# Sixteen-head attention in a decoder: VectorE's instructions pinned to the order of the text, with four of them moved

## The chip, the cores and the metric

The kernel runs on one core of a Trainium2 chip. The metric is the device time of one execution in microseconds (us), the median of three runs. The engines of the core are named as the profile names them: PE is the matrix engine (PEld its weight loads), DVE the vector engine, ACT the scalar (activation) engine, POOL the general one, SP the engine that issues most of the transfers. Each engine works through its own list of instructions in order, and engines wait for each other through semaphores. Matrix products land in PSUM[...].

## The reference

Twelve layers follow each other on x, which is 8 x 256 x 256 (batch, position, width) in float32: four times a self-attention, a cross-attention to a context, and a feed-forward part. After each, x becomes layernorm(x + part). The self-attentions of layers 0, 3 and 6 have 16 heads of width 16, and they are what the change is in; that of layer 9, with heads of width 64, is another function:

```python
# layer 0, 3 and 6, per batch entry and head (d = 16)
s = (q @ k.T) * 0.25          # 0: plain; 3: plus a bias linear in the distance; 6: causal mask
a = softmax(s)                # exp(s - max) / sum
y = concat_heads(a @ v) @ wo  # layers 0 and 3 have biases, layer 0 and 3 also bo
x = layernorm(x + y)
```

## The kernel before

`attention16` computes one such layer; it is called for layers 0 (`kind="bias"`), 3 (`"alibi"`) and 6 (`"causal"`). The work is cut in 16 blocks, `(b, c)`: eight batch entries, and for each the two halves c of eight heads. A block has four steps, s = 0 to 3. `step(i, s)` does two things at once: for the next block i + 1 the scores of four head pairs with queries as rows (tile `s`), from which DVE takes the maximum of each row (line 409; in the causal layer a mask addition, line 401, and two maxima, lines 404 and 406), and for the block i itself the scores with keys as rows (tile `t`), from which the maximum has been taken off already inside the product, and of which ACT makes exponentials (`eT`, line 415). The maxima of a block are collected in `nm`, turned by PE (`ntr`) and put into the queries by `less_max` (`qm`, line 434, two instructions). `attend` multiplies the exponentials with the values and with columns of ones (`av`): the first half of `av` holds the result, the second the sums. `normalise` (lines 462 and 463) takes the reciprocal of the sums and multiplies.

`s` and `t` come from one pool of two buffers of two PSUM banks each, and alternate. So the product `s` of a step can't start before DVE has taken the maximum of the step before it, and `t` not before ACT has made that step's exponentials. The other four banks are two called `av` and two called `mm`; the projections (`pk`, `pq`, `pv`), the output projection `po`, and both kinds of transposes (`ntr`, `xtr`) take turns in the two `mm` banks.

Between the steps stands work of other batch entries: in a block with c = 0 the projections `pk` and `pq` of the next entry and, after step 3, `leave` of the previous entry, which is the output projection (`project_out`, y at line 294) and the norm; in a block with c = 1 the rest of the previous block's attention, `normalise`, the projection `pv`, and `finish` of the previous entry, which transposes the new x for the next layer (`transpose_x`, copied out of PSUM by `evac`).

The norm of one entry is a chain over two engines: DVE makes statistics (lines 158 and 159, two halves of the entry), POOL makes the reciprocal of the deviation (lines 161 and 163), and DVE scales (line 181, two instructions).

The order of PE's instructions in this stage is that of the text: `in_order` ties each matmul and transpose to the one before it, from `chain[:] = [True, None]` to `chain[:] = [False, None]`. All other engines' instructions are put in order by the scheduler of the framework, from its own estimates. `evac` sends every third copy of the whole kernel to ACT and the others to DVE, by a count that runs on through all layers (`turn`).

## Time and profile before

| | |
|---|---|
| median of 3 runs | 4036.28 us (4034.14 to 4036.88) |
| the profiled execution | 4028.63 us, of which the span from first to last instruction is 4026.7 us |
| mean granted PE clock over the span | 0.952 |
| PE busy in 0 to 240 us (layer 0) | 203.16 us; DVE 138.62, ACT 90.07, POOL 23.51; clock 0.95 |
| PE busy in 1055 to 1310 us (layer 3) | 219.11 us; DVE 171.63, ACT 67.70, POOL 15.80; clock 0.91 |
| PE busy in 1955 to 2230 us (layer 6) | 229.04 us; DVE 183.57, ACT 82.85, POOL 62.72; clock 0.90 |

The page gives shares of the whole span; the change concerns these three stretches, so the stretches are what to look at. In them PE is busy most of the time but not all of it, and the clock is below 1. Where a row has "[idle before <-releaser]", the engine stood still for that long before the row, until the named engine had done the named thing.

### The profile page before, as it was taken

Reading aid. Unit: us, or ns where it says so; the run is one execution under the profiler, and the core shown is the slowest. Engines: PE = TensorE matmul, PEld = TensorE weight load, DVE = VectorE, ACT = ScalarE, POOL = GpSimd, SP = SyncE. Lnnn points to the kernel's source line nnn. Section 1 sums busy time; section 2 is a strip of 40 time slices with the busy share of each in tenths; the row PEclk is TensorE's granted clock in tenths of the full one; section 3 lists DMA queues with packets and bytes.
Section 4 is the critical chain, followed back from the end, with each engine's and each line's share of the span. In section 5 each row is a group of like instructions: output and inputs, shape, how many; then the busy total and the mean of one; then the engine's idle time right before and its main releaser. Section 6 shows DMA issues by size and latency. Waiting matters only on the chain.

```text
span 4026.7 us, 51285 instructions
## 1 busy us (share of the span) xinstructions
PE 3652.1 (91%) x21150; PEld 2595.8 (64%) x21150; DVE 1794.2 (45%) x3431; ACT 1057.0 (26%) x2524; POOL 838.3 (21%) x877
## 2 busy tenths in 40 slices
PE   7889999999988787777788999999999999999997
PEld 5557555555555554666655666677776776778886
DVE  4654222222576675111476446766665444420002
ACT  3321111111122232222232332143333333321111
POOL 1000000000000554100122331032223333332213
PEclk9998999999998898788898999999999999999998
DMA  7000000000000000322100400000001000035542
GB/s 258 1 14 7 16 16 16 32 21 15 20 1 12 17 3 21 132 91 89 45 1 1 87 1 22 29 1 1 1 1 40 11 1 11 11 123 183 183 143 64
DMA packets 64714, 175.70 MB, mean 44 GB/s; under 512 B 7808, under 2 KB 39297, under 8 KB 52129
## 3 DMA queue, kind: packets, MB, share of 16 engines
q0 software_dynamic: 16512, 98.38, 6.7%
q1 hardware_dynamic: 47968, 74.05, 6.2%
q8 instruction: 166, 2.72, 0.3%
q14 instruction: 68, 0.55, 0.0%
HBM read 139.12 MB, written 33.29 MB: 43 GB/s over the span
## 4 chain that ended last, share of the span: by engine, by line
PE 43%; DVE 5%; issue 1%; POOL 1%; ACT 1%; another core or an unknown queue 0%; DMA 0%; POOLq 0%; DVEq 0%; ACTq 0%
PE pq L140 4%; PE po L140 4%; PE pv L140 4%; PE ph L1362 4%; PE py L1369 4%; PE s L577 4%; PE av L603 4%; PE pk L140 3%; PE etr L537 3%; PE py_s L1369 1%; PE py L710 1%; PE ph_s L1362 1%; PE ph L725 1%; PE t L140 1%; DVE s L401 1%
## 5 line engine op out<-in xcount | busy, mean ns | idle before, releaser
L529 POOL TENSOR_TENSOR ex<-ex,urc 128x1024 f32<-128x1024 f32 x192 | 363.8, 1895 | 790.5 <-DVE urc L528 709.5
L525 ACT ACTIVATE ex<-s,nm 128x256 f32<-128x256 f32 (+1 forms) x704 | 338.6, 495 | 408.9 <-DVE nm L520 367.5
L415 ACT ACTIVATE eT<-t 128x1024 f32<-128x1024 f32 (+1 forms) x192 | 182.9, 954 | 423.4 <-PE t L140 423.3
L140 PE MATMUL s<-qk,qk 32*128 32x256 f32 (+1 forms) x1536 | 225.5, 414 | 50.4 <-DVE nm L409 42.5
L520 DVE TENSOR_REDUCE nm<-s 128x4 f32<-128x1024 f32 (+1 forms) x192 | 234.1, 1220 | 71.6 <-PE s L577 67.6
L725 PE MATMUL pu<-xT_l,w2a 128*128 128x512 f32 x512 | 244.4, 600 | 0.0
L725 PE MATMUL pg<-xT_l,w2a 128*128 128x512 f32 x512 | 240.8, 592 | 0.0
L851 DVE TENSOR_TENSOR h<-pu,sg 128x512 f32<-128x512 f32 x128 | 88.5, 692 | 337.8 <-PE pu L725 337.7
L140 PE MATMUL t<-qm,qk 32*128 32x256 f32 (+1 forms) x1536 | 213.8, 401 | 23.9 <-DVE nm L406 22.3
L710 PE MATMUL py<-w2b,h 128*128 128x256 f32 x1024 | 226.2, 379 | 0.0
L850 ACT ACTIVATE sg<-pg 128x512 f32<-128x512 f32 x128 | 76.4, 598 | 566.3 <-PE pg L725 566.3
L710 PEld LDWEIGHTS py<-w2b,h 128*128 128x128 f32 x1024 | 194.6, 190 | 40.1 <-issue 15.3
L537 PE MATMUL etr<-ident,ex 128*128 128x128 f32 x1536 | 210.1, 279 | 10.4 <-issue 4.1
L537 PEld LDWEIGHTS etr<-ident,ex 128*128 128x128 f32 x1536 | 169.2, 141 | 71.1 <-issue 57.3
L140 PEld LDWEIGHTS s<-qk,qk 32*128 32x128 f32 x1536 | 130.6, 199 | 125.6 <-DVE nm L409 60.8
L409 DVE TENSOR_REDUCE nm<-s 128x4 f32<-128x1024 f32 x128 | 156.2, 1223 | 107.5 <-PE t L140 78.7
L603 PE MATMUL av<-eT,vg 128*64 128x256 f32 x1280 | 193.1, 394 | 11.4 <-DVE eT L150 10.0
L161 POOL TENSOR_SCALAR ve_l<-mv_l 128x2 f32<-128x2 f32 x104 | 23.3, 224 | 848.8 <-DVE mv_l L159 848.3
L1082 PE MATMUL ph<-xT_l,w 128*128 128x256 f32 x512 | 135.3, 431 | 65.2 <-DMA w<-in_L_ffn_w,row 65.2
L577 PE MATMUL s<-kg,qg 64*128 64x256 f32 x1280 | 190.6, 404 | 2.1 <-DVE eT L150 1.3
L717 DVE SCALAR_TENSOR_TENSOR x<-py,g,x 128x256 f32<-128x256 f32 x256 | 110.2, 479 | 166.1 <-PE py L710 165.9
L725 PEld LDWEIGHTS pu<-xT_l,w2a 128*128 128x128 f32 x512 | 98.1, 192 | 122.1 <-issue 121.9
(337 smaller groups left out, 6690.6 us busy)
## 6 DMA issues: line engine op xcount, KB each, us to landing
slots<-zero SPq DMA_DIRECT2D x16, 1024.0 KB
given<-yo SPq DMA_DIRECT2D x23, 256.0 KB
w2a<-in_L_ffn_Wg SPq DMA_DIRECT2D x8, 512.0 KB
w2a<-in_L_ffn_Wu SPq DMA_DIRECT2D x8, 512.0 KB
w2b<-in_L_ffn_Wd SPq DMA_DIRECT2D x8, 512.0 KB
lines<-w9r SPq DMA_DIRECT2D x1, 4096.0 KB
bias<-lines SPq DMA_DIRECT2D x4, 768.0 KB
x<-in_x SPq DMA_DIRECT2D x8, 256.0 KB
```

Source lines behind the costliest of these rows:

```text
L140: in_order(nc.tensor.matmul(*args, **kw))
L415: nc.scalar.activation(eT[:, :, :n], tt[:, :, :n], AF.Exp)
L520: nc.vector.tensor_reduce(nm[:, :nseg], flat, AX.X, ALU.max, negate=True)
L525: nc.scalar.activation(ex[:, g, :], flat[:, g, :], AF.Exp, bias=nm[:, g:g + 1], accum_out=sums[:, g:g + 1])
L529: nc.gpsimd.tensor_tensor(ex, ex, rc[:, :nseg].unsqueeze(2).to_broadcast([P, nseg, n]), ALU.mult)
L537: nc.tensor.transpose(tr[:, i // 4, (i % 4) * P:(i % 4 + 1) * P], blk, ident)
L577: nc.tensor.matmul(st[:, i, q * S:(q + 1) * S], qg[r:r + d, c, q * P:(q + 1) * P], kg[r:r + d, c, :], start=True, stop=True)
L603: nc.tensor.matmul(av[64 * i:64 * i + d, c * S:(c + 1) * S], vg[:, k, (2 * c + i) * d:(2 * c + i + 1) * d], eT[:, (2 * i + k) * S:(2 * i + ...
L710: nc.tensor.matmul(py[:, q * D:(q + 1) * D], h[:, f, i * P:(i + 1) * P], w2[:, f, :], start=(f == 0), stop=(f == nf - 1))
L725: nc.tensor.matmul(ph, w1[:, c, f * P:(f + 1) * P], xT[p][:, c, :], start=(c == 0), stop=(c == 1))
L1362: nc.tensor.matmul(ph[:, i * S:(i + 1) * S], w1[:, c, f * P:(f + 1) * P], srcs[c], start=(c == 0), stop=(c == 1))
L1369: nc.tensor.matmul(py[:, q * D:(q + 1) * D], h[:, f, q * P:(q + 1) * P], w2[:, f, :], start=(f == 0), stop=(f == NF - 1))
```

## The change

Five edits, all in effect only inside `attention16`:

1. Inside the stage each DVE instruction is tied to the one before it in the text, as PE's are (`order_of_text` names both engines, and `dve` is a wrapper that records each call). The text is rearranged to the order that is wanted.
2. The norm is cut in `norm_stats` and `norm_scaled`. The scaling of an entry is issued after the maximum of step 0 of the next block, no longer before it. The addition of x (`add_x`) stands between the two instructions of `less_max`, the statistics behind the second.
3. `normalise` works on halves of 128 columns: the first half stands in front of a step's maximum (`first` in `step`), the second behind it. For blocks with c = 0 this is step 1 of the block that follows, for blocks with c = 1 step 0 of the block that follows.
4. The copies out of PSUM of `pk`, `pq` and `pv` are issued one step later than their products (`leave_qk`, `leave_v`).
5. The copy of the transposed x goes to ACT always, and takes no turn in the count of `evac`.

PE's instructions in the three layers, and their order, are the same as before.

```diff
+    @contextmanager
+    def order_of_text(*engines):
+        chains.update({e: None for e in engines})
+        yield
+        chains.clear()
...
+        if chains:
+            nc.scalar.copy(dst, src)
+        else:
+            evac(dst, src)
...
+    def norm_stats(b, y, name):
+        return (b, y) + rstd_of([y[:, q, :] for q in range(NT)], f"{name}_{b}")
+
+    def norm_scaled(of):
+        b, y, mv, rs = of
+        for q in range(NT):
+            dve.tensor_scalar(xs[b][:, q, :], y[:, q, :], mv[:, q, 0:1], rs[:, q:q + 1],
+                                    ALU.subtract, ALU.mult)
...
                 for group in products:
                     for o, l, r in group:
                         matmul(o, l, r, start=True, stop=True)
+                first()
...
-                av = avs.pop(i)
-                rc = wk.tile([P, S], F32, tag="rc", name=f"rc_{li}_{b}_{c}")
-                nc.vector.reciprocal(rc, av[:, S:])
-                nc.vector.tensor_tensor(aTs[b][:, c, :], av[:, :S], rc, ALU.mult)
...
+                av = avs[i]
+                lo, hi = half * P, (half + 1) * P
+                rc = wk.tile([P, P], F32, tag="rc", name=f"rc_{li}_{b}_{c}{half}", bufs=4)
+                dve.reciprocal(rc, av[:, S + lo:S + hi])
+                dve.tensor_tensor(aTs[b][:, c, lo:hi], av[:, lo:hi], rc, ALU.mult)
...
+                for i, (b, c) in enumerate(blocks):
+                    more = b + 1 < B
+                    if c == 0:
+                        step(i, 0, lambda: normalise(i - 1, 0))
+                        normalise(i - 1, 1)
+                        if more:
+                            pk = project_qk(b + 1, 1)
+                        step(i, 1)
+                        if more:
+                            leave_qk(b + 1, 1, pk)
+                            pq = project_qk(b + 1, 0)
+                    else:
+                        step(i, 0)
+                        if b > 0:
+                            norm_scaled(ys.pop(b - 1))
+                        attend(i - 1, 1, (1,))
+                        step(i, 1, lambda: normalise(i - 1, 0))
+                        normalise(i - 1, 1)
+                        if more:
+                            pv = proj_tok(wv, xTb(b + 1), 0, f"pv_{li}_{b + 1}")
+                    step(i, 2)
                     if more:
+                        if c == 0:
+                            leave_qk(b + 1, 0, pq)
+                        else:
+                            leave_v(b + 1, pv)
+                    attend(i, 0, (0, 1))
+                    step(i, 3)
+                    if b > 0:
+                        if c == 0:
+                            po = project_out_mm([aTs.pop(b - 1)], wo, f"{li}_{b - 1}")
+                        else:
+                            finish(b - 1, f"l{li}", last)
+                    if i + 1 < len(blocks):
+                        tr = turn_maxima(i + 1)
+                        less_max(i + 1, 0, tr)
+                    if b > 0 and c == 0:
+                        y = add_x(wk, b - 1, po, bo, f"{li}_{b - 1}")
+                    if i + 1 < len(blocks):
+                        less_max(i + 1, 1, tr)
+                    if b > 0 and c == 0:
+                        ys[b - 1] = norm_stats(b - 1, y, f"l{li}")
+                    attend(i, 1, (0,) if c == 0 else (0, 1))
```

## The prediction

> **What bounds the kernel now.** The page first: its shares and its clock row.

> ```profile
> span 4026.7 us, 51285 instructions
> ...
> PE 3652.1 (91%) x21150; PEld 2595.8 (64%) x21150; DVE 1794.2 (45%) x3431; ACT 1057.0 (26%) x2524; POOL 838.3 (21%) x877
> ...
> PEclk9998999999998898788898999999999999999998
> ```

> PE sets the end nearly everywhere, so time can be won in two ways only: PE stands still less, or it is granted its clock more. The change acts in three stretches (layer 0, about 20 to 277 us; layer 3, 1054 to 1310; layer 6, 1960 to 2218), and there the clock row is lowest. So next, who PE waits for, in the even part of each stretch (90 to 235, 1100 to 1273, 2005 to 2180 us):

> ```profile
> PE s L140 <- DVE nm L409: 12.9, 11, 2.1
> ...
> PE s L140 <- DVE nm L409: 15.2, 13, 2.1
> ...
> PE t L140 <- DVE nm L406: 19.3, 12, 2.5
> ```

> Columns: us in total, times, longest. PE waits for DVE's maximum, because it frees the buffer of the next product. Third, the timeline of layer 0 around the longest of these waits, DVE and PE:

> ```profile
> 103.69 0.48 DVE L434 SCALAR_TENSOR_TENSOR qm<-ntr,hc,qk 128x256 f32<-128x256 f32 x1
> 104.08 0.74 DVE L158 BATCH_NORM_STATS2 st_l<-y 128x6 f32<-128x256 f32 x2
> ...
> 105.19 0.17 DVE L159 BATCH_NORM_AGGREGATE mv_l<-st_l 128x2 f32<-128x6 f32 x1
> 106.51 0.73 DVE L181 TENSOR_SCALAR x<-y,mv_l,rs_l 128x256 f32<-128x256 f32 x2 [1.15 <-POOL rs_l L163]
> 107.16 1.22 DVE L409 TENSOR_REDUCE nm<-s 128x4 f32<-128x1024 f32 x1
> ...
> 108.44 0.64 PE L140 MATMUL s<-qk,qk 32*128 32x256 f32 x2 [2.08 <-DVE nm L409]
> ```

> The scores were ready at 105.33, but DVE, in order, waits 1.15 us for POOL's part of the norm, scales for 0.73, and only then takes the maximum; PE has nothing from 106.36 on. Last, the clock around it, by windows of 3.4 us (us; busy us of PE, PEld, DVE, ACT, POOL; PE clock; DMA share; GB/s):

> ```profile
> 105.20:108.60 3.40, 1.32 (x24) 0.58 (x24) 2.25 (x6) 1.02 (x1) 0.94 (x2) 1.00 0.00 0
> 108.60:112.00 3.40, 3.40 (x20) 2.38 (x21) 3.00 (x3) 1.03 (x1) 0.00 (x0) 0.51 0.02 5
> 112.00:115.40 3.40, 3.40 (x45) 2.19 (x48) 2.02 (x5) 1.02 (x1) 0.00 (x0) 0.99 0.00 0
> ```

> After the stall PE runs at half clock for one such window. So the stall is paid twice.

> **The change part by part.** I count against the profiled execution: span 4026.7 us, its own time 4028.63 (1.9 around the span), 7.7 below the median of the runs. A saving in the span is taken off the median unchanged.

> *The maximum before the scaling.* One batch entry (two blocks) takes 30.26 us in layer 0 (such a stall ends at 108.44, the next at 138.70). In the new order DVE runs qm, y, qm, statistics, then the maximum. Laid out with the rows' durations: ntr ends at 103.26; qm (0.48) to 103.79; y (0.69) to 104.42; the second qm (0.46) to 104.83; two statistics of 0.42 and two aggregates of 0.17, each waiting for the one before, to 105.95; maximum (1.22) to 107.12; PE goes on at 107.2 instead of 108.44. Saved 1.23, left over 0.84. The order of y and qm costs half a microsecond of what taking out 1.15 + 0.73 should give. POOL's part (0.23 and 0.71) now runs beside the maximum and is done by about 107.1, so the scaling no longer waits; it is late by a maximum, but its reader, the transpose in `finish`, comes after step 3, 10 us later. Occurrences: six in layer 0 (79.55 to 229.5) and six in layer 3 (1112.4 to 1260.7), 2 x 6 x 1.23 = 14.8. In layer 6 the stall is 2.49: the same layout ends the statistics at 76.2 (of 2076.2) where the mask addition started at 2077.59, so 1.44 each, x 6 = 8.6. Sum 23.4.

> *Reciprocals in halves.* Rows, DVE by form:

> ```profile
> L462 DVE RECIPROCAL rc<-av 128x256 f32<-128x256 f32 x48 | 84.2, 1754 | 26.7 <-PE av L140 26.7
> L528 DVE RECIPROCAL urc<-us 128x4 f32<-128x4 f32 x160 | 28.2, 176 | 110.0 <-ACT ex L525 108.3 <-issue 0.6
> ```

> The trace has no reciprocal of 128 columns. By these two, (1754 - 176) / 252 = 6.26 ns a column, so 0.95 us (estimate); the multiplication by the 128-column row of line 361 is 0.28, where 256 take 0.42. A half costs 1.23, both 2.46 instead of 2.18. The maximum of step 0 in blocks with c = 0 now waits for 1.23 instead of 2.18, 0.95 earlier. PE's wait there is 0.47 (at 124.25, after pk) in layers 0 and 3 and 0.79 in layer 6: it goes entirely. 6 x (0.47 + 0.47 + 0.79) = 10.4, and in the last entry, with no projection to fill in (gap 2.40 at 243.95), 0.95 in each layer, 2.9. The second half stands before the next maximum, but that maximum's scores come only after another step of PE: from 123.2 it ends at 124.4, the scores at about 124.9, so it is covered by 0.5 us; a half over 1.7 us would stall there. [...] The row gives this cost, about 0.15 us (what is left of 176 ns at four columns). [...] If that lay on the path, it would take 3 x 7 x 0.6 = 12.6 from the gain; DVE is busy 18.90 of 30 us (104 to 134), so I take nothing in the even part and 0.3 us at each layer's end, where `normalise` has no cover.

> *The clock.* The half-clock windows behind these stalls: four in layer 0 (from 108.6, 139.4, 170.1, 200.8), four in layer 3 (1142.9, 1200.9, 1231.6, 1262.4), eight in layer 6 between 2020 and 2177. Their price shows in layer 3, where two entries have none and take 28.82 us and the others 30.20: 1.4 each. In layer 6 an entry with two windows takes 31.24, with one 30.24: 1.0. 8 x 1.4 + 8 x 1.0 = 19.2. Does a stall of 0.84 (1.05 in layer 6) still trip it? Windows in which PE stood still up to 1.31 us kept the clock (57.5 to 60.9 us: 2.08 of 3.40 busy), those over 1.9 lost it, between there are both. So I count all of it. [...]

> *Copies a step later, and x's copy to ACT.* pk and pq are left by ACT in layers 0 and 6 and by DVE in layer 3 (0.74 x 4 per entry); all are still a step ahead of the product that reads them. pv's copies (0.88) go behind a maximum that follows at once. The `mm` bank of each is wanted again two banks later. ACT takes 0.59 where DVE took 0.69; ACT idles over half of the time here, and the copied x is read in the next layer. I count nothing, with one exception: from layer 1 on the count of `evac` stands elsewhere, and the copy of layer 1's last x falls to ACT, behind a table load (1.28) and an activation (0.55), with the router waiting: 2 us. No SP transfer is added, removed or moved, and POOL keeps its work, but for the place of a few small instructions.

> Sum: 23.4 + 10.4 + 2.9 + 19.2 = 55.9, less 0.9 and 2: **53 us**, a span of 3974 and a median of **3983**. Bounds: if the waits in question go in full (6 x (2.07 + 0.47) twice, 6 x (2.49 + 0.79), clock 19, ends 3), 72, so 3964; if the clock still halves and the last two edits cost 5 more, 29, so 4007.

> **The rivals.** What a measurement can tell from no change is about 0.2%, 8 us.

> - *The clock still halves* (left-over idle of 0.84 adds to the 0.73 at ntr or to short gaps in one window): 53 - 19 = 34, 4002. For it: windows with 1.42 and 1.44 us of idle did lose it in layer 6. Against: the two gaps are 8 us apart.
> - *PE becomes the bound* in the stage, because the statistics are quicker than laid out or ACT's relief shifts everything forward: 72 us, 3964. Against: DVE's chain from ntr to the maximum has no slack in it.
> - *It does nothing*, as the scheduler's order was the text's: 4036. Against: in the listing of both programs the maximum and the scaling do change places and the halves are there.
> - *Slower, by the count of `evac`.* 24 copies no longer count, so in layers 4, 7, 9 and 10 another third of the 192 large copies (eT, 1213 ns on DVE, 1013 on ACT) goes to ACT. If that breaks a tight rhythm there, each unit pays; from 53 / 192 = 0.28 us a unit on it eats the gain, and at 0.33 the time is 4046. For it: ACT and DVE both serve the softmax there. Against: PE is busy at 8 tenths or more there, and its waits for DVE are short.

> **How the numbers follow.** Chances: the forecast 0.68 (its own range 3966 to 3998), the clock 0.14, PE the bound 0.08, no effect 0.04, slower 0.06 with half of it within 8 us or so of no change. Faster by over 0.2%: 0.68 + 0.14 + 0.08 + 0.02 = 0.92; same 0.04; slower 0.04. The range reaches from 3958, a little below the bound of 3964, to 4007, the bound with the clock lost.

> **What would show it.** Right: in layer 0 the wait of `s` after the norm near 0.8 us and none after pk; the scaling with no wait for POOL; entries of 27 us in layer 0 instead of 30.26, and 28 in layer 6; clock 1.00 between 100 and 230 us; reciprocals near 0.95 us. Wrong: half-clock windows once per entry as before, halves well over 1 us, or the three stretches shorter while the later ones, above all 1310 to 1590 and 2218 to 3550 us, are longer.

## The result and the profile after

The changed kernel takes 3975.17 us (median of four runs, 3971.26 to 3978.78), the kernel before 4035.21 on the same chip: a ratio of 0.9852, with a 95% interval of 0.9835 to 0.9869, so 60 us or 1.5% faster. The forecast was 3983. The profiled execution took 3973.46 us, its span is 3971.8, which is 54.9 less than the span of before; the working had found 53. The two numbers agree better than the reasons do, as will be seen.

The page of the changed kernel, shares and clock row:

```profile
span 3971.8 us, 51356 instructions
...
PE 3625.3 (91%) x21150; PEld 2579.6 (65%) x21150; DVE 1799.3 (45%) x3511; ACT 1062.2 (27%) x2540; POOL 836.7 (21%) x877
...
PEclk9998999999999998887999999999999999999998
```

PE has the same 21150 instructions and is busy 26.8 us less: they did not become fewer, more of them run at the full clock (the mean granted clock is 0.952 before and 0.959 now). The page's clock row is too coarse to show where: in layers 0 and 3 it has nines before and after. (The prediction called it lowest in the three stretches. That was misread: it is lowest, with a 7, in layer 5, which the change does not touch; of the three only layer 6 has eights.) The answer by windows shows it, for layers 0, 3 and 6 of the kernel before and of the changed kernel (us; busy us of PE, PEld, DVE, ACT, POOL; PE clock; DMA share; GB/s):

```profile
0.00:277.00 277.00, 229.91 (x2404) 147.10 (x2405) 155.60 (x227) 98.64 (x134) 25.37 (x55) 0.94 0.27 99
1054.00:1310.00 256.00, 220.11 (x2356) 137.56 (x2354) 172.63 (x257) 67.70 (x67) 16.11 (x24) 0.91 0.02 6
1960.00:2218.00 258.00, 212.04 (x2354) 149.49 (x2353) 178.41 (x319) 80.22 (x130) 58.66 (x150) 0.91 0.01 2
```

```profile
0.00:254.00 254.00, 217.87 (x2404) 139.80 (x2405) 157.48 (x254) 100.79 (x139) 25.33 (x55) 0.97 0.30 108
1036.00:1267.00 231.00, 208.35 (x2352) 131.30 (x2352) 174.09 (x283) 70.00 (x72) 16.31 (x25) 0.96 0.02 6
1920.00:2157.00 237.00, 206.78 (x2356) 145.52 (x2357) 179.04 (x346) 80.56 (x133) 58.65 (x146) 0.93 0.01 3
```

The clock is 0.97, 0.96 and 0.93 there, where the kernel before has 0.94, 0.91 and 0.91. DVE has 80 instructions more: 96 additional halves, less the 16 copies of x that ACT took over. In the three layers all of DVE's rows now carry line 150, the wrapper that records them, and are told apart by their tiles.

Who PE waits for in the even part of layers 0, 3 and 6 of the changed kernel (85 to 215, 1085 to 1240, 1980 to 2115 us; total, times, longest, in us):

```profile
PE ntr L158 <- DVE nm L150: 3.6, 5, 0.7
PE s L155 <- DVE nm L150: 3.4, 5, 0.7
...
PE s L155 <- DVE nm L150: 5.5, 7, 1.5
...
PE t L155 <- DVE nm L150: 5.8, 6, 1.1
```

The wait of 2.1 us for the maximum is now one of 0.7, and the wait of 2.5 in layer 6 one of 1.1. (The single wait of 1.5 in the second answer, which is layer 3's, belongs to the last batch entry.) The wait is not gone. Why it is what it is shows in the timeline of layer 0, the rows of DVE, POOL and PE around one of these waits:

```profile
101.45 0.48 DVE L150 SCALAR_TENSOR_TENSOR qm<-ntr,hc,qk 128x256 f32<-128x256 f32 x1 [0.97 <-PE ntr L158]
101.86 0.68 DVE L150 TENSOR_TENSOR y<-po,xb 128x512 f32<-128x512 f32 x1
102.45 0.48 DVE L150 SCALAR_TENSOR_TENSOR qm<-ntr,hc,qk 128x256 f32<-128x256 f32 x1
...
102.84 0.42 DVE L150 BATCH_NORM_STATS2 st_l<-y 128x6 f32<-128x256 f32 x1
...
103.83 0.18 DVE L150 BATCH_NORM_AGGREGATE mv_l<-st_l 128x2 f32<-128x6 f32 x1
103.92 1.19 DVE L150 TENSOR_REDUCE nm<-s 128x4 f32<-128x1024 f32 x1
...
104.40 0.71 POOL L178 TENSOR_TENSOR rs_l<-ve_l,nhalf 128x2 f32<-128x2 f32 x1
105.15 0.74 DVE L150 TENSOR_SCALAR x<-y,mv_l,rs_l 128x256 f32<-128x256 f32 x2
105.17 0.48 PE L155 MATMUL s<-qk,qk 32*128 32x256 f32 x2 [0.68 <-DVE nm L150]
```

From the end of `ntr` (101.41) to the end of the maximum (105.11) DVE is never idle for longer than a hand-over (0.04 us), and POOL's part of the norm (done at 105.11) lies wholly beside the maximum: the row of the scaling shows no wait any more. The clock behind this stall, in two windows (columns as above):

```profile
102.80:106.20 3.40, 2.72 (x48) 1.42 (x40) 3.30 (x9) 1.02 (x1) 2.03 (x3) 1.00 0.02 5
106.20:109.60 3.40, 3.37 (x35) 2.33 (x34) 3.28 (x6) 1.06 (x2) 0.00 (x0) 1.00 0.00 0
```

PE idles 0.68 us in the first, and the second is granted 1.00. Before, the idle was 2.08 and the next window got 0.51. The halves of `normalise`, DVE by form:

```profile
L150 DVE RECIPROCAL rc<-av 128x128 f32<-128x128 f32 x96 | 91.3, 951 | 30.9 <-PE av L155 30.9
...
L150 DVE TENSOR_TENSOR aT<-av,rc 128x128 f32<-128x128 f32 x96 | 28.0, 291 | 3.3
```

0.951 and 0.291 us, where 0.95 and 0.28 were worked out.

**Where the time went, layer by layer.** A layer is taken to end with PE's last transposition of x (`xtr`) in it. By these marks layers 0, 3 and 6 take 276.7, 256.3 and 257.9 us before, and 253.6, 231.2 and 236.5 after: 69.7 less together. The other nine took 14.8 more: layer 1 1.3, layer 2 3.9, layer 4 3.3, layer 7 2.1, layer 9 1.0, layer 10 6.1, layer 5 3.3 less, and the rest next to nothing. Inside the three layers the period from one batch entry to the next (from `ntr` to `ntr`) went from 29.99 to 26.76 us, from 29.94 to 26.70 and from 30.72 to 27.58 in the mean of the last five; the seven periods of each layer, summed, are 55.6 us shorter over the three. The rest of the 69.7, 14 us, came in the last entries.

### The profile page after: what moved, and what is told of

Its sections match the earlier page's. It is cut to its first block, busy times and chain, and to the rows that moved or that the text cites. A ratio compares the mean times of both kernels' runs of the same rounds, so it can differ in the third digit from the quotient of the medians.

```text
span 3971.8 us, 51356 instructions
## 1 busy us (share of the span) xinstructions
PE 3625.3 (91%) x21150; PEld 2579.6 (65%) x21150; DVE 1799.3 (45%) x3511; ACT 1062.2 (27%) x2540; POOL 836.7 (21%) x877
## 4 chain that ended last, share of the span: by engine, by line
PE 45%; DVE 4%; issue 1%; POOL 1%; ACT 1%; another core or an unknown queue 1%; DMA 0%; POOLq 0%; DVEq 0%; ACTq 0%
PE pq L155 4%; PE po L155 4%; PE s L629 4%; PE ph L1414 4%; PE py L1421 4%; PE pv L155 4%; PE pk L155 4%; PE av L655 4%; PE etr L589 3%; PE py_s L1421 1%; PE py L762 1%; PE ph_s L1414 1%; PE ph L777 1%; PE av L155 1%; PE t L155 1%
## 5 line engine op out<-in xcount | busy, mean ns | idle before, releaser
L150 DVE TENSOR_REDUCE nm<-s 128x4 f32<-128x1024 f32 (+2 forms) x256 | 221.4, 887 | 86.6 <-PE t L155 56.8
L155 PE MATMUL s<-qk,qk 32*128 32x256 f32 (+1 forms) x1536 | 215.7, 400 | 25.8 <-DVE nm L150 19.1
L589 PE MATMUL etr<-ident,ex 128*128 128x128 f32 x1536 | 212.2, 281 | 12.6 <-POOL ex L581 5.7
L155 PE MATMUL t<-qm,qk 32*128 32x256 f32 (+1 forms) x1536 | 205.8, 389 | 9.9 <-DVE nm L150 8.6
L655 PE MATMUL av<-eT,vg 128*64 128x256 f32 x1280 | 193.8, 396 | 11.4 <-DVE eT L150 10.0
```

The source lines that it names most:

```text
L150: return lambda *args, **kw: in_order(getattr(nc.vector, op)(*args, **kw))
L155: in_order(nc.tensor.matmul(*args, **kw))
L589: nc.tensor.transpose(tr[:, i // 4, (i % 4) * P:(i % 4 + 1) * P], blk, ident)
L655: nc.tensor.matmul(av[64 * i:64 * i + d, c * S:(c + 1) * S], vg[:, k, (2 * c + i) * d:(2 * c + i + 1) * d], eT[:, (2 * i + k) * S:(2 * i + ...
```

## The experiments

They ran on three other chips, four experiments on each: those of the first three headings on the first; the fill, the first pair for the count of the copies and the later statistics on the second; the rest on the third. There the kernel before takes 3999.36, 3998.59 and 4002.32 us, not 4035; the last section says where the difference lies. Ratios are to the kernel before on the same chip. The changed kernel itself was run again on the second and the third of these chips (0.9869 and 0.9849), not on the first. What the copies that are issued a step later and the copy of x on ACT (edits 4 and 5, apart from the count of the copies) are worth was not tested by a run of its own.

### The maximum ahead of the scaling, undone

```diff
-                        step(i, 0)
-                        if b > 0:
-                            norm_scaled(ys.pop(b - 1))
+                        step(i, 0, lambda: b > 0 and norm_scaled(ys.pop(b - 1)))
```

> The new kernel with one thing undone: the scaling of the norm again stands before the maximum of step 0 (the halves, the pinned order and the copies stay). My theory: the wait for POOL and the scaling in front of the maximum, with the half clock that follows, are the larger part of the gain (23.4 + 19.2 of 55.9 us), so this kernel comes out near 3975 + 42 = 4017 us, and its trace shows a wait of `s` of 2 us and a half-clock window once per entry in layers 0 and 3. Rival: the halves and the pinning bring it, the scaling's place is a detail; then it stays under 3990.

Measured: 3997.94 us, ratio 0.9991 (0.9984 to 0.9998). All of the gain is gone: by the changed kernel's ratios on the other two chips this is 51 to 59 us above it, where 42 were expected. Who PE waits for in layer 0 of this kernel, 85 to 235 us:

```profile
PE s L155 <- DVE nm L150: 12.9, 5, 2.6
```

2.6 us each, half a microsecond more than before the change (there were 2.1), since y and the statistics now stand where the text puts them. The half-clock windows are back as well: 9, 9 and 18 in the three layers (counted in windows of 3.41 us, the start of the layers among them), where the changed kernel has 4, 5 and 9.5 and the kernel before 10, 13 and 15. Entries take 29.87, 29.83 and 30.75 us, as before the change to within 0.13 us. So without this move nothing is left of the gain. It does not follow that the move alone makes it. Put back in this way, the stall is 0.5 us longer than the old one, and the count of the copies stays shifted (below): layers 2 and 4 take 8.7 us more than in the kernel before, while layers 0, 3 and 6 together take 12.3 less. And the next runs show that the move needs the other edits.

### The reciprocals whole again

```diff
-                lo, hi = half * P, (half + 1) * P
-                rc = wk.tile([P, P], F32, tag="rc", name=f"rc_{li}_{b}_{c}{half}", bufs=4)
+                if half == 1:
+                    return
+                lo, hi = 0, S
+                rc = wk.tile([P, S], F32, tag="rc", name=f"rc_{li}_{b}_{c}{half}", bufs=4)
```

> The new kernel with the reciprocals whole again, in the place of the first half. My theory: what was 0.47 us after pk (0.79 in layer 6) comes back, six times a layer, and 0.95 at each end: 13 us, so 3988, and no half-clock windows in layers 0 and 3. Rival: the whole reciprocal, in front of a maximum in every block, makes stalls long enough to lose the clock too; then over 4000.

Measured: 3970.7 us, ratio 0.9916 (0.9899 to 0.9932). The changed kernel itself has 0.9869 and 0.9849 on the two other chips, so the halves are worth some 19 to 27 us here, more than the 13 expected. Gap by gap, PE waits 0.67 us after the attention, 0.47 after `pk`, and a third time after `pv`, where the changed kernel does not wait at all and the kernel before at most 0.18 us. Rows of DVE and PE in layer 0 of this kernel:

```profile
106.71 0.74 DVE L150 TENSOR_SCALAR x<-y,mv_l,rs_l 128x256 f32<-128x256 f32 x2
106.73 0.48 PE L155 MATMUL s<-qk,qk 32*128 32x256 f32 x2 [0.67 <-DVE nm L150]
107.36 1.75 DVE L150 RECIPROCAL rc<-av 128x256 f32<-128x256 f32 x1
107.81 1.99 PE L155 MATMUL pv<-w0a,xT_in 128*128 128x256 f32 x8
109.15 0.42 DVE L150 TENSOR_TENSOR aT<-av,rc 128x256 f32<-128x256 f32 x1
109.49 1.22 DVE L150 TENSOR_REDUCE nm<-s 128x4 f32<-128x1024 f32 x1
110.76 0.48 PE L155 MATMUL s<-qk,qk 32*128 32x256 f32 x2 [0.96 <-DVE nm L150]
```

This is where the stall goes when the scaling is moved and the reciprocals stay whole. The scaling (0.74) now stands between two maxima, and with a whole reciprocal and its multiplication behind it (1.75 and 0.42) the second maximum is late by 0.96. In the kernel before the reciprocal stood in the same place, but without the scaling in front of it: there PE waited 0.18 us after `pv` in the entries at full clock (`pv` 1.99 us, as at 80.63), and not at all where `pv` ran at half clock (2.84 us, at 110.31). 0.47 + 0.96 = 1.43 is nearly the whole difference of an entry, 28.23 us against 26.76. So of what the halves are worth, the larger part is not the wait that they mend but the one that the moved scaling would have made.

### The order pinned, with the old text; and the new text with only PE pinned

The first keeps the body of the layer as it was before the change and only records DVE's calls, all of them, for the tie:

```diff
-                    nc.vector.scalar_tensor_tensor(qm, tr[:, :S], hc[:, 2 + e:3 + e],
+                    dve.scalar_tensor_tensor(qm, tr[:, :S], hc[:, 2 + e:3 + e],
...
-            chain[:] = [True, None]
+            chains.update({mybir.EngineType.PE: None, mybir.EngineType.DVE: None})
...
```

> The kernel before with one edit alone: DVE tied to the order of its own old text (no piece moved, cut or delayed). My theory: pinning gives nothing by itself; in the old text the qk and v copies and the norm stand before maxima, so it is no faster than before, 4035, and rather slower, up to 4080. Rival: the scheduler's order was the trouble, and following the text is enough; then under 4000.

The second is the changed kernel without the tie of DVE:

```diff
-            with order_of_text(mybir.EngineType.PE, mybir.EngineType.DVE):
+            with order_of_text(mybir.EngineType.PE):
```

> The new text with PE alone tied to it; the scheduler orders DVE again. My theory: the scheduler by its own estimates puts the scaling back before the maximum, so most of the gain goes: 4015 or more. Rival: the new text is enough, since the scheduler follows it where its estimates tie; then within 10 us of 3975.

Measured: 4049.71 us (ratio 1.0113, 1.0096 to 1.0130) and 4012.6 us (1.0031, 1.0022 to 1.0040). Each half of the edit alone is slower than the kernel before, by 50 and 13 us (the second with the shifted count of the copies, which is taken up below). Two answers for layer 0, 85 to 235 us, first the old text pinned, then the new text with DVE left to the scheduler:

```profile
PE t L155 <- DVE qm L150: 9.7, 4, 2.4
...
PE s L155 <- DVE nm L150: 3.1, 7, 0.5
```

```profile
PE s L155 <- DVE nm L150: 14.8, 11, 2.1
```

In the old text `leave` stands ahead of `less_max`, so pinned, y and the norm delay `qm`, and PE waits 2.4 us for that. With DVE free, the scheduler puts the scaling ahead of the maximum again: in the trace DVE waits 1.15 us for POOL before it (at 109.29), and PE 2.15 us for the maximum (at 111.22). The gain belongs to the order, and an order that is only written and not tied is not kept.

### How much of it is the clock

The kernel before, with four products put in that nobody reads (a constant tile times the identity, 2.0 us of PE, work that the reference doesn't ask for), at the place where PE stood still for 2.1 us:

```diff
+            cmask2 = wk.tile([P, S], F32, tag="fill", name=f"fill{li}", bufs=1)
+            nc.gpsimd.memset(cmask2, 1.0)
...
                     attend(i - 1, 1, (1,))
+                    if b > 0:
+                        fl = bank("mm", f"fl_{li}_{b}")
+                        for _ in range(4):
+                            matmul(fl[:, :S], ident, cmask2, start=True, stop=True)
                     normalise(i - 1)
```

> The kernel before, with four matmuls of 128x256 that nobody reads put into the stall, seven times a layer, so that PE isn't idle there; no wait is taken away. It does useless work besides the reference's. It measures the clock alone. My theory: each half-clock window behind a stall costs 1.0 to 1.4 us, 19 us in all; the fillers' ends cost up to 0.3 us each (6): 13 to 19 us faster than before, 4016 to 4022, with few half-clock windows in the three stretches. Rival[...]: no gain, 4035 or more.

Measured: 3989.76 us, ratio 0.9977 (0.9968 to 0.9987): useless work makes the kernel 9 us faster, less than the 13 to 19 expected. A stall of before with the fill in it (columns as above), and PE's waits in layer 0, 85 to 235 us:

```profile
105.00:108.40 3.40, 3.40 (x39) 2.33 (x40) 2.25 (x8) 1.02 (x1) 1.74 (x3) 1.00 0.02 7
108.40:111.80 3.40, 3.24 (x26) 2.31 (x25) 3.37 (x4) 1.02 (x1) 0.00 (x0) 1.00 0.00 0
```

```profile
PE ntr L143 <- DVE nm L411: 4.4, 6, 0.7
PE s L140 <- DVE nm L411: 3.4, 11, 0.5
```

Maximum and scaling are as before; only the idle time is filled, and the clock stays. The periods between entries show the price most cleanly. Before, they are 28.98, 30.27, 30.26, 30.31, 30.25, 28.88 us in layer 0, and with the fill 28.97, 28.88, 28.87, 28.88, 28.87, 28.88. The entries that had no half-clock window did not change, the four others lost 1.4 us each. Over all periods of the three layers the fill takes off 5.6, 5.6 and 7.6, together 18.8 us. That the whole gains 9 only is due in part to the starts and ends of the three layers, which are 2.9 us longer with the fill, and in part to other layers: layer 4, in which nothing was changed, has 17.2 half-clock windows in this profile and 13.3 in that of before, and is 6.0 us longer.

### The changed kernel once more, and with the count of the copies kept

```diff
         if chains:
+            turn[0] += 1
             nc.scalar.copy(dst, src)
```

> The new kernel unchanged, as the yardstick of this series on the same chip: 3975 us, within 4.

> The new kernel, but the copies of the transposed x to ACT keep their turns in the count of evac, so that every later copy goes to the same engine as in the kernel before. In the two profiles the untouched layers together are 15 us longer after the change. My theory: the shifted count makes about half of that (the last copy of layer 1 behind ACT's table load, and layer 10), so this kernel is 5 to 10 us faster than the new one. Rival: the untouched layers differ by where the clock's windows fall, not by the count; then within 3 us of the new kernel.

> The kernel of e6 again, as the measure for e9 and e10 on the same chip; about 13 us shorter than the kernel after on the chip of e5 and e6, 1.6% below the kernel before.

> The kernel after on the same chip. The count of the copies is the only difference to e11: about 9 us of PE standing still longer by the traces (4 in layer 2, 5 in layer 4), so 5 to 13 us longer than e11. If the 13 us of e6 were clock alone, there would be no fixed difference.

Measured on the second chip 3948.55 (ratio 0.9869, 0.9853 to 0.9885; 3975 was expected from the first chip, and the last section says where the chips differ) and 3935.53 with the count kept (0.9845, 0.9832 to 0.9859); on the third 3943.31 (0.9849, 0.9836 to 0.9863) and 3935.24 (0.9833, 0.9819 to 0.9846). So the kernel with the shifted count is slower by 13 and 8 us; the intervals of each pair overlap, but the two pairs agree in sign, and the traces show a place for a part of it. In all seven profiles with the count as before, PE stands still for 5.9 us in layer 1, for 2.6 to 2.9 in layer 2 and for 61 to 63 in layer 4; in all seven with it shifted, for 6.9 to 7.0, 4.4 and 65.5 to 67. PE's waits in layer 4 of the pair on the third chip (1260 to 1560 us), count kept and count shifted:

```profile
PE qtr L1014 <- POOL raw L995: 10.1, 2, 6.3
...
PE s L1036 <- ACT ex L578: 5.5, 3, 2.0
```

```profile
PE qtr L1013 <- POOL raw L994: 11.8, 2, 6.0
...
PE s L1035 <- ACT ex L577: 7.6, 4, 2.0
```

And in the changed kernel, at the border of layers 1 and 2 (345 to 372 us), the wait that the prediction had named, behind ACT's activation:

```profile
PE pg L777 <- ACT sg L902: 1.1, 1, 1.1
```

Together 8 us of standstill (1.1 + 1.8 + 5) and one half-clock window more in layer 2 (6.9 instead of 5.9), with the count shifted. The lengths of the layers bear this out in layer 2 (684.3 to 685.7 us, and 688.8 to 689.3 shifted); in layer 4, where the half-clock windows vary from 12 to 17, the two kinds overlap and differ by 3 us in the mean. So some 8 us can be put on the count. In both pairs another 6.4 us or so lie in layers 7, 8 and 9. PE stands still there for at most 0.4 us more; what is seen to differ is the clock (in layer 7 2.5 half-clock windows in the changed kernel, where the kernel before has 1.2). Four other kernels with the shifted count do not have it (layer 7 takes 246.3 to 246.5 us in them, 249.0 in the changed kernel), and the old text pinned, with the count as before, does (248.9). So this part, like the differences of layer 5, is not shown to be from the count, and its cause stays open.

### The rest of the stall

What is left are 0.68 us at step 1. If it is DVE's time ahead of the maximum, moving the statistics behind it should help:

```diff
                         step(i, 0)
                         if b > 0:
-                            norm_scaled(ys.pop(b - 1))
+                            of = norm_stats(b - 1, ys.pop(b - 1), f"l{li}")
                         attend(i - 1, 1, (1,))
                         step(i, 1, lambda: normalise(i - 1, 0))
+                        if b > 0:
+                            norm_scaled(of)
                         normalise(i - 1, 1)
...
-                        ys[b - 1] = norm_stats(b - 1, y, f"l{li}")
+                        ys[b - 1] = y
```

> The new kernel with the statistics of the norm too behind the maximum of step 0, and the scaling behind that of step 1. My theory: what is left of the stall (0.68 us in layers 0 and 3, 1.12 in layer 6) is the statistics in front of the maximum, so it goes: 6 x (0.68 + 0.68 + 1.12) = 15, and 4 half-clock windows in layer 6, 4 to 5: 3955 to 3960. Rival: the statistics then stand before the reciprocals and the maximum of step 1, and the stall moves there; within 5 us of the new kernel or slower.

Measured: 3940.0 us (ratio 0.9854, 0.9839 to 0.9869), but the entries take 26.71, 26.66 and 27.44 us, at most 0.14 less than in the changed kernel. In layer 0, 85 to 235 us:

```profile
PE s L155 <- DVE nm L150: 5.9, 12, 1.5
```

Twelve waits instead of seven, 5.9 us in all where the changed kernel has 6.2: the 0.68 became 0.32 at step 1 and 0.31 at step 2, since the 1.17 us of statistics now stand ahead of the next maximum. The 8.6 us that the medians gain are for the most part not from this stall; layers 5, 7 and 9, which the edit does not touch, are 3.1, 2.5 and 1.9 us shorter (the last section tells how the half-clock windows of layers 5 and 7 vary). So only one half of the statistics was moved, with the count kept (`half_stats` is `bn_stats` and `bn_aggr` of one half; POOL's two instructions follow the second):

```diff
                         step(i, 0)
                         if b > 0:
-                            norm_scaled(ys.pop(b - 1))
+                            y, st, mv = ys.pop(b - 1)
+                            half_stats(y, 1, st, mv)
...
                         attend(i - 1, 1, (1,))
                         step(i, 1, lambda: normalise(i - 1, 0))
+                        if b > 0:
+                            norm_scaled(of)
...
-                        ys[b - 1] = norm_stats(b - 1, y, f"l{li}")
...
+                        half_stats(y, 0, st, mv)
+                        ys[b - 1] = y, st, mv
```

> The kernel after, with the count of the copies kept as in the run e6, one half of the norm's statistics (0.6 us of DVE) ahead of the maximum of step 0 and the other half behind it, and the scaling behind the maximum of step 1. If what is left of the stall is DVE's time ahead of that maximum and nothing else, half of the statistics leaves it: the wait of s falls from 0.68 to about 0.1 us, no new wait comes at step 1 (with both halves moved, in e8, it was 0.31), an entry takes 26.2 us instead of 26.76 in layers 0 and 3 and about 27 in layer 6, and the whole is 3 x 7 x 0.58 = 12 us shorter than the run with the count kept beside it. Rival: DVE's list between the two maxima is full, the stall only changes its place as in e8; then an entry stays at 26.7 and the two runs are within 4 us of each other.

Measured: 3926.41 us, ratio 0.9811 (0.9798 to 0.9825), 8.8 us less than the kernel with the count kept, on the same chip, where 12 were expected; the two intervals overlap. Entries take 26.30 us in layer 0 and 26.25 in layer 3, 0.45 less than with the statistics in one piece; in layer 6 the mean of the last five is 27.37, against 27.40. One row of the timeline:

```profile
131.69 0.48 PE L155 MATMUL s<-qk,qk 32*128 32x256 f32 x2 [0.32 <-DVE nm L150]
```

0.32 are left, not 0.1: the maximum itself takes longer (1.23 us and the hand-over) than the half of the attention that PE has to do meanwhile (1.05), so 0.3 would stay with DVE idle ahead of it. That was left out of the expectation. Nothing new appeared at step 2. But the 8.8 us are not these entries. The seven periods of each layer are together 6.4 us shorter in the profile, and the three layers as wholes only 1.7: half-clock windows fell at their starts and ends (layer 0 has 6.8 instead of 3.3). Of the 11.4 us between the two profiled spans 9.7 lie in layers that the edit does not touch. So the shorter entries of layers 0 and 3 are shown; that the whole gains by them is not. Last, the wait of 0.73 us at `ntr`, which every kernel had:

```diff
+                    if c == 1:
+                        attend(i, 1, (0,))
                     if i + 1 < len(blocks):
                         tr = turn_maxima(i + 1)
...
-                    attend(i, 1, (0,) if c == 0 else (0, 1))
+                    attend(i, 1, (0,) if c == 0 else (1,))
```

> As e9, and in blocks with c = 1 half of the attention's products (16, 1.07 us) stand ahead of the turned maxima, no longer behind them. PE waits 0.73 us for the maximum there, once per entry, in every kernel so far. The products need the exponentials, which end 0.15 us before the maximum; so if the wait is only a matter of what PE is given to do, it falls to some 0.3 us and the whole is 3 x 7 x 0.4 = 8 us shorter than e9. Rival: the product t of the next step needs the queries less their maxima, which now come 1.07 us later, and the wait goes there: no change, or up to 6 us longer.

Measured: 3928.93 us, ratio 0.9813 (0.98 to 0.9827), no difference to the one before it, where 8 us were expected.

```profile
PE av L155 <- ACT eT L454: 3.5, 6, 0.6
```

Now PE waits 0.58 us at the same place for ACT's exponentials, which end only 0.15 us before the maximum, and an entry takes 26.30 us as before. The 0.15 us that the wait lost come back as PE's own work, 25.40 us in an entry instead of 25.26; why is not known. The kernel with the split statistics and the count kept has the lowest median of all, 1.9% below the kernel before, where the change alone is 1.5% below it; between it and the kernel with the count kept alone (1.7%) the noise decides.

## Why the prediction came out right

**The stall.** The step "saved 1.23, left over 0.84" gave the mechanism and nearly the size: 1.39 saved and 0.68 left in layers 0 and 3, because the second `qm` and the statistics follow each other a little more closely than laid out (3.70 us from `ntr` to the end of the maximum, not 3.86); in layer 6 1.37 saved instead of 1.44 (the two times that the prediction gives there differ by 1.39). The waits of 0.47 and 0.79 went entirely, as said. With six occurrences each, the waits sum to 6 x (1.39 + 0.47) x 2 + 6 x (1.37 + 0.79) = 35.3 us, where 33.8 were counted. The run with the scaling put back shows that the gain is not there without this move, and the row of the scaling, which no longer waits for POOL, shows how.

**The clock.** 19.2 us were counted for half-clock windows in the even part; the fill, which changes nothing but the idle time, takes off 18.8 there. With the 2.1 us of idle filled, the window behind is granted 1.00, where it had 0.51; so the half clock came from the idle time, and was paid on top of it. The step was too generous in one place: in layer 6 left-over stalls of 1.1 us still trip it in most entries, which take 27.77 us there and 26.85 where they don't, so its six entries gained 18.2 us and not the 21.4 counted. Layers 0 and 3 gained more than counted instead, 18.4 us each and not 15.8: an entry that had been at full clock went from 28.88 to 26.75 us, by 2.13, of which 1.86 are the two waits (1.70 were counted) and 0.18 the wait after `pv`, which the prediction had left out. So, with the first entries, the even part came to 55.6, against 53.0; that these errors cancel in part is luck.

**What was mis-sized.** Two terms, and that they offset each other is luck. The first is "2.9 in the last entries, less 0.9 for `normalise` without a cover": the ends of the three layers gained 14 us. The last wait fell from 2.40 to 1.46, as worked out; but in the kernel before there were half-clock windows at the end too, which the count of windows had left out. Here are two of them, in layer 0 of the kernel before:

```profile
244.40:247.80 3.40, 2.09 (x28) 1.50 (x24) 1.23 (x1) 1.02 (x1) 0.00 (x0) 0.61 0.00 0
247.80:251.20 3.40, 3.40 (x36) 1.38 (x32) 1.23 (x1) 1.03 (x1) 0.00 (x0) 0.50 0.00 0
```

In the profile of the changed kernel the same part of the last entry has none: it takes 13.15 us from one `ntr` to the next in layers 0 and 3, before 16.73 and 18.01. That is not fixed either: in the profile of the same program on the third other chip layer 3 takes 16.14 there, so some 3 of the 14 us are where the windows happened to fall. What follows it to the end of the layer is also shorter, by 2.0, 1.5 and 0.9 us.

The second term is "2 us" for the copies and the count of `evac`. The other layers took 14.8 us more, which is what the prediction had named as a sign of its being wrong; the pairs with and without the count differ by 8 and 13 us, of which some 8 can be put on the count. The rival "slower, by the count" had named the mechanism, with the 192 large copies in layers 4, 7, 9 and 10 at up to 0.28 us each; what the traces show is 5 us in layer 4 and 3 in layers 1 and 2, but 0.4 in layer 9 and none in layer 7. It was real and too small to decide. The rest of the 14.8 is mostly the clock in layers that were not touched (in layer 10 PE is busy for 466.59 us at 0.97, before for 462.48 at 0.98); 4.9 us of layer 10's 6.1 were not seen again in the two later profiles of the same program (483.9 us each, where the first has 488.8) and stay unexplained.

So 53 was right as 56 + 14 - 15. The medians differ by 60 and not by 54.9, since the profiled execution of before lies 6.6 us below the median of 4035.21, and that of after 1.7 below its own. The chances that the prediction drew from its list do not follow from it: by the list, faster has 0.90, the same 0.07 and slower 0.03.

**The other steps.** "A half reciprocal 0.95 us" holds (0.951). The cost that each instruction more adds, 0.15 us by the prediction's row (four more in an entry are its 0.6 us), holds for a reciprocal of 128 columns too: twice 0.951 less 1.754 is 0.15 us for one more; two halves with their multiplications take 2.48 us of DVE, the whole 2.18. It did not matter, as argued, since DVE had room (19.10 us busy in the 26.76 of an entry, 104 to 130.76 us); the run with the whole reciprocals shows that short ones are what the order needs. That step was right for another reason than it gave: it counted the waits that were there, and said nothing of the 0.96 us after `pv` that whole reciprocals would have made in the new order. "PE becomes the bound" did not come: 0.68 and 0.73 us per entry still wait for DVE. "The clock still halves" is right in layer 6 only.

## What to carry to other kernels

When a serial engine frees the buffer that the bounding engine waits for, put that instruction first in its list and everything with slack behind it, in pieces no longer than the gap between two such instructions; and tie the order: left free, the scheduler put the scaling back in front of the maximum here. Count a stall of the matrix engine twice where the clock row dips behind it (here 2.08 us of idle, and 1.4 us more by the window at half clock), and look at the ends of each stage too. A counter that runs through the whole program and deals out work by turns makes distant stages depend on an edit here: keep it in step.

## What was not expected of the hardware

**The clock of layers that nobody touched.** Layer 5 takes 355.0 to 358.4 us, with 34.8 to 38.8 half-clock windows, layer 7 246.2 to 249.0 with 0.8 to 2.5, in kernels whose text is the same there, while PE stands still equally long (96.6 to 97.7 us, and 12.3 to 12.4). The changed kernel alone has 355.0, 358.4 and 355.7 us for layer 5 in its three profiles. Differences of a few us between two kernels can be this alone; the run with the later statistics is an example, and the trace, not the median, showed it.

**The last layer differs between chips.** It takes 476.5 and 476.7 us in the two kernels on the first chip, and 450.8 on the three others (449.3 in one run). On the first, PE stands still before `py_s`, in the changed kernel for 7.9 and 9.2 us; the rows of the first of these waits:

```profile
3898.07 0.60 ACT L1416 ACTIVATE h_s<-ph_s 128x512 f32<-128x512 f32 x1 [20.38 <-remote]
...
3898.72 2.08 PE L1421 MATMUL py_s<-w11b_s,h_s 128*128 128x256 f32 x4 [7.86 <-ACT h_s L1416]
```

ACT begins late, and the trace doesn't say what it waited for; in the changed kernel on the second of the other chips PE waits for it 0.6 us in all. If the kernel before takes as long for this layer on the others as every kernel traced there, it explains 26 of the 36 us by which that kernel differs between the chips. It is the reason why every ratio here is taken on one chip.
